# Two images, two stages at once: additive attention of one image beside the experts of the other

## The chip, the cores and the metric

The kernel runs on one core of one Trainium2 chip. The metric is the device time of one execution in microseconds (us). The core has five engines that take their instructions from queues of their own, in order: TensorE (PE in the profile; its weight loads are PEld), VectorE (DVE), ScalarE (ACT), GpSimd (POOL) and SyncE (SP), which here only starts transfers. POOL starts the indirect transfers (gathers and scatters by a list of rows).

## The reference, cut to what matters

The input is x with 2 images, 256 channels and 32 x 32 positions, in float32. Four layers follow each other. Layers 0 and 1 are attention over channels-first images and are not touched. Layers 2 and 3 work on tokens, 1024 an image, 256 values each:

```python
t = _to_tokens(x)
t = t + _L2_attn_ref(_ln_t(t), ...)      # attention in windows of 64 tokens
t = t + _L2_ffn_ref(_ln_t(t), ...)       # 8 experts, top 2, hidden width 1024
t = t + _L3_attn_ref(_ln_t(t), ...)      # additive attention, within one image
t = t + _L3_ffn_ref(_ln_t(t), ...)       # 8 experts, top 2, hidden width 512

# _L3_attn_ref, U = 32 units
q = inputs @ Wt;  k = inputs @ Wx
h = tanh(q[:, :, None, :] + k[:, None, :, :] + bh)   # 2 x 1024 x 1024 x 32 values
a = softmax(h @ Wa + ba);  v = a @ inputs

# an expert layer, for each token and its two experts
h = gelu(xf @ W1 + b1);  y = h @ W2 + b2;  out = sum of weight * y
```

Every step here works within one image, so the two images do not depend on each other from layer 2 on.

## The kernel before, in words

All matrix work is float32. A tile is 128 tokens; there are 16 (NT), eight an image. Each stage treats both images and ends before the next one begins, because the next norm needs its result. From layer 2 on the order is: norm, `window_attention`, norm, `route`, `experts` (layer 2), norm, `additive_attention`, norm, `route`, `experts` (layer 3) with `finish`, which writes the output.

*Experts.* `route` computes the gate, picks two experts a token and gives every token-expert pair a row ("slot") in a buffer in HBM, sorted by expert and padded so that a tile of TILE = 256 slots belongs to one expert: NTILES = 23 tiles. The tokens are scattered to `slots_in` by 32 indirect transfers (L934). For each tile, `fetch` gathers the whole weights of its expert with one indirect transfer (L952: 2.10 MB in layer 2, 1.05 MB in layer 3) and loads the tokens on SP (L964); `turn` transposes them (L973) and in layer 2 applies the expert's scale and shift on VectorE (L979); `up` does the first matrix product (L992) and `gelu` on ScalarE with the bias in the same instruction (L996); `down` does the second product (L1005), VectorE copies it (L1009) and SP stores it to `slots_out` (L1010). The weights have three buffers. The order of this loop is fixed by hand: within `tc.manual_schedule()` every engine's queue has the order in which the program emits. Elsewhere a scheduler orders the instructions by priority (the order of the program) and by its own estimate of when they are ready. At the end 32 gathers (L1031) bring the two results of each token back, and VectorE adds them with their shares (L1035).

*Additive attention.* Keys lie with 32 units x 4 copies on the partitions, so one ScalarE instruction computes tanh for 4 queries against 1024 keys (L1109). A step is four of these; after eight steps a tile of 128 queries is done. TensorE sums over the units with the matrix `pick` (L1115, four column groups of 32); VectorE takes the maximum (L1120), ScalarE the exponential (L1125), TensorE transposes (L1133), VectorE copies (L1135), TensorE multiplies with the tokens (L1138), VectorE adds to t (L1142). The norms take their root on ScalarE (L79).

Of the kernel before, what the change touches and what calls it, by code (L numbers as in the profile page):

```python
# [19 lines left out]
F32 = mybir.dt.float32  # L20
U32 = mybir.dt.uint32
# [15 lines left out]
TILE = 256  # L37

NTILES = 2 * T // TILE + E - 1
MASKED = -1.0e30  # L40

# [6 lines left out]
class Stack:  # L48
# [351 lines left out]
    def layer0(self, xT):  # L400
        tc, nc = self.tc, self.nc
        with ExitStack() as ctx:
# [106 lines left out]
            for m in range(NTILES * TILE // P):  # L509
                nc.gpsimd.dma_start(out=self.slots_in[m * P : (m + 1) * P, :], in_=zero)  # L510
# [165 lines left out]
    def window_attention(self, t, u, uT):  # L676
# [124 lines left out]

    def route(self, pool, psum, uT, wr, br, normalise):

        nc = self.nc  # L810
        shape = [P, NT, E]
        tl = lambda name, s=shape, dt=F32: pool.tile(s, dt, name=name)
        ps = psum.tile(shape, F32, name="ps_router", tag="tr")
        for i in range(NT):
            for c in range(CC):
                nc.tensor.matmul(
                    ps[:, i, :], lhsT=uT[:, c, i * P : (i + 1) * P], rhs=wr[:, c, :],
                    start=(c == 0), stop=(c == CC - 1),
                )
        iota = lambda t, pattern, base, step: nc.gpsimd.iota(  # L820
            t, pattern=pattern, base=base, channel_multiplier=step, allow_small_or_imprecise_dtypes=True
        )
        rank, limits, tiles, part = tl("rank", [P, E]), tl("rt_lim", [P, E]), tl("rt_til", [P, NTILES]), tl("rt_part", [P, 1])
        iota(rank, [[-1, E]], E, 0)
        iota(limits, [[TILE, E]], 0, 0)
        iota(tiles, [[1, NTILES]], 0, 0)
        iota(part, [[0, 1]], 0, 1)

        before, ones = tl("rt_before", [P, P]), tl("rt_ones", [P, P])
        nc.gpsimd.memset(ones, 1.0)  # L830
        nc.gpsimd.affine_select(
            before, ones, pattern=[[1, P]], compare_op=ALU.is_ge, fill=0.0, base=-1, channel_multiplier=-1
        )
        over_tokens = lambda a, s=shape: a.unsqueeze(1).to_broadcast(s)
        one = tl("rt_one", [P, NT])
        lg, p, eq, h0, h1 = (tl(f"rt_{n}") for n in ("lg", "p", "eq", "h0", "h1"))
        nc.vector.tensor_tensor(lg, ps, over_tokens(br), ALU.add)
        nc.vector.tensor_reduce(one, lg, AX.X, ALU.max)
        nc.vector.tensor_tensor(lg, lg, broadcast(one, shape), ALU.subtract)
        nc.scalar.activation(lg, lg, AF.Exp)  # L840
        nc.vector.tensor_reduce(one, lg, AX.X, ALU.add)
        nc.vector.reciprocal(one, one)
        nc.vector.tensor_tensor(p, lg, broadcast(one, shape), ALU.mult)
        left = p
        for hot in (h0, h1):
            nc.vector.tensor_reduce(one, left, AX.X, ALU.max)
            nc.vector.tensor_tensor(eq, left, broadcast(one, shape), ALU.is_equal)
            nc.vector.tensor_tensor(eq, eq, over_tokens(rank), ALU.mult)
            nc.vector.tensor_reduce(one, eq, AX.X, ALU.max)
            nc.vector.tensor_tensor(hot, over_tokens(rank), broadcast(one, shape), ALU.is_equal)  # L850
            if hot is h0:
                nc.vector.scalar_tensor_tensor(lg, hot, -2.0, p, ALU.mult, ALU.add)
                left = lg
        both = eq
        nc.vector.tensor_tensor(both, h0, h1, ALU.add)


        flat = lambda a: a.rearrange("p n e -> p (n e)")
        inside = psum.tile(shape, F32, name="ps_before", tag="before")
        nc.tensor.matmul(flat(inside), lhsT=before, rhs=flat(both), start=True, stop=True)  # L860
        counts = psum.tile(shape, F32, name="ps_counts", tag="counts")
        nc.tensor.matmul(flat(counts), lhsT=ones, rhs=flat(both), start=True, stop=True)
        a, b, n = tl("rt_a"), tl("rt_b"), 1
        nc.vector.tensor_copy(a, counts)
        while n < NT:
            nc.vector.tensor_copy(b[:, :n], a[:, :n])
            nc.vector.tensor_tensor(b[:, n:], a[:, n:], a[:, : NT - n], ALU.add)
            a, b, n = b, a, 2 * n
        total = a[:, NT - 1, :]
        over, need = tl("rt_over", [P, E, E]), tl("rt_need", [P, E])  # L870
        nc.vector.tensor_tensor(
            over, broadcast(total, [P, E, E]), over_tokens(limits, [P, E, E]), ALU.is_gt
        )
        nc.vector.tensor_reduce(need, over, AX.X, ALU.add)
        ends, spare, n = tl("rt_ends", [P, E]), tl("rt_spare", [P, E]), 1
        nc.vector.tensor_copy(ends, need)
        while n < E:
            nc.vector.tensor_copy(spare[:, :n], ends[:, :n])
            nc.vector.tensor_tensor(spare[:, n:], ends[:, n:], ends[:, : E - n], ALU.add)
            ends, spare, n = spare, ends, 2 * n  # L880
        nc.vector.tensor_tensor(spare, ends, need, ALU.subtract)
        nc.vector.tensor_scalar(spare, spare, float(TILE), None, ALU.mult)
        nc.vector.tensor_tensor(b, a, counts, ALU.subtract)
        nc.vector.tensor_tensor(b, b, inside, ALU.add)
        nc.vector.tensor_tensor(b, b, over_tokens(spare), ALU.add)
        slots, shares = [], []
        for n, hot in enumerate((h0, h1)):
            nc.vector.tensor_tensor(lg, hot, b, ALU.mult)
            nc.vector.tensor_reduce(one, lg, AX.X, ALU.add)
            slots.append(tl(f"rt_slot{n}", [P, NT], U32))  # L890
            nc.vector.tensor_copy(slots[n], one)
        whose, index = tl("rt_whose", [P, NTILES, E]), tl("rt_index", [P, NTILES])
        shape_t = [P, NTILES, E]
        nc.vector.tensor_tensor(whose, over_tokens(ends, shape_t), broadcast(tiles, shape_t), ALU.is_le)
        nc.vector.tensor_reduce(index, whose, AX.X, ALU.add)
        nc.vector.tensor_scalar(index, index, float(E - 1), float(P), ALU.min, ALU.mult)
        nc.vector.tensor_scalar(index, index, part, None, ALU.add)
        rows = tl("rt_rows", [P, NTILES], U32)
        nc.vector.tensor_copy(rows, index)

        nc.vector.tensor_tensor(p, p, both, ALU.mult)
        if normalise:
            nc.vector.tensor_reduce(one, p, AX.X, ALU.add)
            nc.vector.reciprocal(one, one)
            nc.vector.tensor_tensor(p, p, broadcast(one, shape), ALU.mult)
        for n, hot in enumerate((h0, h1)):
            nc.vector.tensor_tensor(hot, hot, p, ALU.mult)
            shares.append(tl(f"rt_share{n}", [P, NT]))
            nc.vector.tensor_reduce(shares[n], hot, AX.X, ALU.add)
        return p, shares, slots, rows  # L910

    def experts(self, t, u, routes, packed, b2, hid, affine, finish=lambda g: None):

        tc, nc = self.tc, self.nc  # L920
        HB, TB = hid // P, TILE // P
        weights, shares, slots, rows = routes
        width = packed.shape[1]
        with ExitStack() as ctx:
            sb = ctx.enter_context(tc.tile_pool(name="ex_sb", bufs=2))
            wp = ctx.enter_context(tc.tile_pool(name="ex_w", bufs=3))
            p_x = ctx.enter_context(tc.tile_pool(name="ex_x", bufs=2, space=PSUM))
            p_h = ctx.enter_context(tc.tile_pool(name="ex_h", bufs=2, space=PSUM))
            p_y = ctx.enter_context(tc.tile_pool(name="ex_y", bufs=2, space=PSUM))
            xs, ys = self.slots_in, self.slots_out  # L930

            for i in range(NT):
                for slot in slots:
                    nc.gpsimd.indirect_dma_start(  # L934
                        out=xs, out_offset=bass.IndirectOffsetOnAxis(ap=slot[:, i : i + 1], axis=0),
                        in_=u[:, i, :], in_offset=None,
                    )

            for i in range(NT):
                ps = p_y.tile([E, P], F32, name="ps_wT", tag="ps_y")  # L940
                nc.tensor.transpose(ps, weights[:, i, :], self.ident)
# [72 lines left out]
            with tc.manual_schedule():  # L1014
# [4 lines left out]
                for m in range(NTILES):  # L1019
                    if m + 2 < NTILES:  # L1020
                        fetch(m + 2)
# [130 lines left out]
    def run(self):  # L1152
        tc, nc, ins = self.tc, self.nc, self.ins
        with ExitStack() as ctx:
# [29 lines left out]
            def norm(src=t, dst=u, dstT=uT):  # L1184
                self.layer_norm(dst, src, 1e-5)
                if dstT is None:
                    return
# [121 lines left out]
```

## Time and profile before

| | us |
|---|---|
| median of 3 runs | 3524.49 (3524.22 to 3526.67) |
| the profiled execution, own time | 3520.51 |
| its span, first to last instruction | 3518.8 |
| layers 0 and 1, with the turn to tokens | to about 1809 |
| window attention | 1809 to 2003 |
| norm, route, scatters | 2003 to 2142 |
| experts of layer 2 | 2142 to 2497 |
| gathers, norm, projections | 2497 to 2562 |
| additive attention | 2562 to 3138 |
| norm, route, scatters | 3138 to 3268 |
| experts of layer 3 | 3268 to 3468 |
| gathers and output | 3468 to 3519 |

The stages are read from the chain of work that ended last. Over the whole span TensorE is busy 88%, ScalarE 58%, VectorE 49%, POOL 7%. A busy share counts the time in which an instruction of the engine is under way; a matmul counts from its start to its modelled end, so matmuls with waits between them can look like a busy engine. The granted clock of TensorE is given as a share of full speed (mean 0.927 here).

### The profile page before, as it was taken

To read this page: it belongs to the slowest core of one execution; us is meant where nothing else is said; L and a number is where in the kernel's file an instruction comes from. 1 tells how busy PE (TensorE), PEld (TensorE's weight loads), DVE (VectorE), ACT (ScalarE), POOL (GpSimd) and SP (SyncE) were. 2 spreads that over 40 slices of the span, in tenths; PEclk is the share of its full clock that TensorE was granted. 3 is DMA by queue.
4 is the path that set the end of the run, shared out by engine and by line. 5 is a ranking of instruction groups with operands and counts; after the bars stand their busy time and mean duration, and the time that the engine had idled before them with its cause. 6 is when DMAs were issued, how large, how long until landed. Compare 5 with 4: busy or idle time off the path is not lost.

```text
span 3518.8 us, 67832 instructions
## 1 busy us (share of the span) xinstructions
PE 3106.9 (88%) x28148; PEld 1875.6 (53%) x28148; DVE 1725.4 (49%) x3134; ACT 2056.3 (58%) x3148; POOL 259.1 (7%) x411
## 2 busy tenths in 40 slices
PE   7999999999999989999979835999499999982795
PEld 4566665666656656656757714788322222231673
DVE  5989898898988945434545430111321111121112
ACT  2888888787888846646633201222189999950121
POOL 3000000000000000000000021000300000003113
PEclk9999999999999999999987657999799999985897
DMA  3000000000000000000000022444200000002454
GB/s 110 3 3 3 3 3 3 3 3 3 3 3 3 3 25 1 1 1 1 1 19 1 1 102 87 180 173 166 82 1 1 1 1 0 1 1 76 139 183 135
DMA packets 154356, 134.18 MB, mean 38 GB/s; under 512 B 114544, under 2 KB 141056, under 8 KB 148160
## 3 DMA queue, kind: packets, MB, share of 16 engines
q0 software_dynamic: 14976, 95.36, 7.2%
q1 hardware_dynamic: 137632, 34.02, 4.5%
q8 instruction: 221, 3.62, 0.4%
q14 instruction: 87, 0.71, 0.1%
q10 hardware_dynamic: 1440, 0.47, 0.1%
HBM read 100.51 MB, written 28.57 MB: 37 GB/s over the span
## 4 chain that ended last, share of the span: by engine, by line
PE 83%; DMA 6%; DVE 5%; issue 3%; ACT 2%; POOL 1%; SPq 0%; POOLq 0%; ACTq 0%; DVEq 0%
PE ps_s L272 13%; PE ps_o L348 13%; PE ps_e L1115 12%; PE ps_h L992 7%; PE ps_y L1005 7%; DMA slots_in<-u,rt_slot 4%; PE ps_t L330 4%; PE ps_s L143 4%; PE ps_o L210 3%; PE ps_t L173 3%; PE ps_v L1138 2%; PE ps_t L631 2%; PE ps_av L776 1%; DMA got<-slots_out,rt_slot 1%; PE ps_out L526 1%
## 5 line engine op out<-in xcount | busy, mean ns | idle before, releaser
L309 ACT ACTIVATE sc<-sc,sa_shift 128x1024 f32<-128x1024 f32 x512 | 585.2, 1148 | 53.1 <-DMA sa_shift<-sa_min 52.9
L1109 ACT ACTIVATE th<-kT,qb 128x1024 f32<-128x1024 f32 x512 | 535.2, 1134 | 8.5 <-DVE kT L1088 6.9
L272 PE MATMUL ps_s<-kT,qT 64*32 64x512 f32 x8192 | 503.9, 595 | 9.2 <-ACT sc L282 8.5
L348 PE MATMUL ps_o<-wt,v 128*64 128x128 f32 x6144 | 502.2, 276 | 0.0
L1115 PE MATMUL ps_e<-th,pick 128*32 128x512 f32 x2048 | 470.7, 602 | 0.9 <-DVE kT L1088 0.9
L322 DVE STREAM_TRANSPOSE wt<-sc 128x768 f32<-128x768 f32 x512 | 465.7, 943 | 1.0 <-ACT sc L309 1.0
L348 PEld LDWEIGHTS ps_o<-wt,v 128*64 128x64 f32 x6144 | 441.2, 137 | 42.5 <-issue 42.5
L996 ACT ACTIVATE h<-ps_h,w 128x256 f32<-128x256 f32 x276 | 130.6, 473 | 477.2 <-PE ps_h L992 477.2
L282 ACT COPY sc<-ps_s 128x1024 f32<-128x1024 f32 x256 | 257.4, 1005 | 116.1 <-PE ps_s L272 42.4
L293 DVE TENSOR_REDUCE sa_least<-sc 128x1 f32<-128x1024 f32 x256 | 306.1, 1196 | 1.4 <-ACT sc L282 1.3
L279 DVE TENSOR_SCALAR_CACHE_REDUCE sc<-ps_s 128x1024 f32<-128x1024 f32 x256 | 301.3, 1177 | 5.9 <-PE ps_s L272 5.9
L992 PE MATMUL ps_h<-xe,w 128*128 128x256 f32 x1104 | 253.4, 387 | 35.0 <-issue 31.0
L1115 PEld LDWEIGHTS ps_e<-th,pick 128*32 128x32 f32 x2048 | 93.0, 108 | 333.0 <-ACT th L1109 227.1
L1009 DVE COPY y<-ps_y 128x256 f32<-128x256 f32 x92 | 39.0, 424 | 453.3 <-PE ps_y L1005 453.3
L348 PE MATMUL ps_o<-wl,v_odd 128*64 128x128 f32 x2048 | 250.9, 276 | 0.0
L1005 PE MATMUL ps_y<-w,h 128*128 128x256 f32 x1104 | 245.5, 379 | 0.0
L992 PEld LDWEIGHTS ps_h<-xe,w 128*128 128x128 f32 x1104 | 196.5, 191 | 84.8 <-issue 40.6
L149 DVE TENSOR_SCALAR_CACHE_REDUCE sc<-ps_s 128x1024 f32<-128x1024 f32 x128 | 151.6, 1222 | 178.5 <-PE ps_s L143 178.5
L272 PEld LDWEIGHTS ps_s<-kT,qT 64*32 64x32 f32 x8192 | 126.9, 106 | 200.6 <-issue 169.5
L1005 PEld LDWEIGHTS ps_y<-w,h 128*128 128x128 f32 x1104 | 210.2, 190 | 28.1
L330 PEld LDWEIGHTS ps_t<-ident,sc 128*128 128x128 f32 x1024 | 107.3, 140 | 215.7 <-issue 168.5
L348 PEld LDWEIGHTS ps_o<-wl,v_odd 128*64 128x64 f32 x2048 | 220.3, 137 | 0.0
(248 smaller groups left out, 3525.3 us busy)
## 6 DMA issues: line engine op xcount, KB each, us to landing
xr<-slots_in SPq DMA_DIRECT2D x46, 256.0 KB, 2.8
slots_out<-y SPq DMA_DIRECT2D x46, 256.0 KB, 2.2
sa_got<-sa_least SPq DMA_DIRECT2D x512, 0.5 KB, 1.8
sa_shift<-sa_min SPq DMA_DIRECT2D x512, 0.2 KB, 1.7
slots_in<-zero POOLq DMA_DIRECT2D x46, 128.0 KB, 2.2
sa_sums<-sa_total SPq DMA_DIRECT2D x256, 1.0 KB, 1.8
xT<-in_x SPq DMA_DIRECT2D x4, 496.0 KB, 4.2
sb_l_w_in<-in_l_w_in SPq DMA_DIRECT2D x1, 1536.0 KB, 6.3
```

The source lines that it names most:

```text
L272: nc.tensor.matmul(ps[r][S * c : S * (c + 1), a, :].rearrange("p (b i) -> p b i", i=S), lhsT=qT[half, p, S * i : S * (i + 1)], rhs=keys[ha ...
L279: nc.vector.tensor_scalar(scores[m][0], flat[0], 1.0, None, ALU.mult, ALU.min, accum_out=least[m // 2][:, 0, h : h + 1])
L282: nc.scalar.copy(scores[m][1], flat[1])
L293: nc.vector.tensor_reduce(least[m // 2][:, 1, h : h + 1], scores[m][1], AX.X, ALU.min)
L309: nc.scalar.activation(scores[m][r], scores[m][r], AF.Exp, bias=shift[m // 2][:, r : r + 1], scale=-1.0, accum_out=total[i][:, 2 * p + r, ...
L322: nc.vector.transpose(weights[i, h][:, 2 * p + r, :], scores[m][r][:, :DIRECT])
L330: nc.tensor.transpose(ps[:, g, r, :], s[:, at : at + P], self.ident)
L348: nc.tensor.matmul(sums[i][64 * k : 64 * (k + 1)], lhsT=values, rhs=w, start=(h == 0 and j == 0 and t == 0), stop=(h == 1 and j == 1 and t ...
L992: nc.tensor.matmul(ps, lhsT=a[:, c, j * P : (j + 1) * P], rhs=x[:, c, :], start=(c == 0), stop=(c == CC - 1),)
L1005: nc.tensor.matmul(ps, lhsT=h[:, j, k * P : (k + 1) * P], rhs=b[:, j, :], start=(j == 0), stop=(j == HB - 1),)
L1109: nc.scalar.activation(h, keys.rearrange("p (a b) -> p a b", a=2), AF.Tanh, bias=qb[:, i, g : g + 1])
L1115: nc.tensor.matmul(pe[c * U : (c + 1) * U, a, :], lhsT=pick[:, k, :], rhs=h[:, a, :], start=(k == 0), stop=(k == G - 1),)
```

## The change

From layer 2's experts on, each stage is cut by image. A new class `Late` holds the stages as generators that emit a piece of work and yield. `run` gives each one a start, an end and a number of pieces, and emits the pieces of all in the order of these places, all inside one `manual_schedule`. So the experts of image 0 run beside the dispatch (norm, route, scatter) of image 1; the attention of image 0 beside the experts of image 1; the attention of image 1 beside the layer-3 dispatch, experts and collect of image 0; the same for image 1 comes last. The dispatch of image 0 in layer 2 is emitted inside `window_attention`, after the last tile of image 0.

With it come these edits. The expert tile is 128 slots (TILE = 128), with 23 tiles an image. A gelu takes its bias from a VectorE add before it, covers 512 values, and is emitted one `up` later. `fetch`, `turn` and `up` have a new order. Slots have a buffer for each image. The root in the norms is computed on VectorE (`inverse_root`, three Newton steps on the bits), not on ScalarE. The exponentials of attention come in batches of 4, 3 and 1 tiles. The buffer of sums `ps_e` is single, tanh tiles have eight buffers as before. Constants are loaded when layer 2 begins.

```diff
-TILE = 256
-NTILES = 2 * T // TILE + E - 1
+IT = N // P
+TILE = 128
+NTILES = 2 * N // TILE + E - 1
...
+                after(i, lambda shape, name: p_mm.tile(shape, F32, name=name, tag="ps_mm"))
...
+            late = Late(ctx, self, t)
...
+                def after(i, psum):
+                    if i == IT - 1:
+                        late.misc = psum
+                        for _ in late.dispatch(2, 0):
+                            pass
+                self.window_attention(t, u, uT, after)
+            late.run()
...
+    def inverse_root(self, var, eps):
...
+        for step in range(3):
+            nc.vector.scalar_tensor_tensor(a, y, -0.5, y, ALU.mult, ALU.mult)
+            nc.vector.tensor_tensor(a, a, x, ALU.mult)
+            nc.vector.scalar_tensor_tensor(y, a, 1.5, y, ALU.add, ALU.mult)
...
+    def dispatch(self, l, b):
+        for half in range(2):
+            yield from self.normed(b, half)
+        yield from self.route(l, b)
+        u = self.u[b]
+        if l == 2:
+            yield from self.norm(lambda i: u[:, i, :], lambda i: u[:, i, :], range(IT))
+        p, shares, slots, rows = self.routes[l, b]
+        nc, t = self.nc, self.t
+        for i in range(IT):
+            for slot in slots:
+                nc.gpsimd.indirect_dma_start(
+                    out=self.stack.slots_in[b],
...
+        yield
+        for i in range(IT):
...
+            nc.tensor.matmul(ps, lhsT=wT, rhs=self.b2[l], start=True, stop=True)
...
+    def experts(self, l, b):
...
+        def fetch(m):
+            w = sb.tile([P, WIDEST], F32, name="ew", bufs=3)
+            nc.gpsimd.indirect_dma_start(
...
+            raw[m] = sb.tile([P, C], F32, name="xr", bufs=3)
+            nc.sync.dma_start(out=raw[m], in_=xs[m * TILE : (m + 1) * TILE, :])
...
+        def activate():
+            while waiting:
+                to, x = waiting.pop()
+                nc.scalar.activation(to, x, AF.Gelu)
+        def up(m, k):
...
+            h = sb.tile([P, 4, TILE], F32, name="hb")
+            nc.vector.tensor_tensor(h, ps, broadcast(b1[:, 4 * k : 4 * k + 4], [P, 4, TILE]), ALU.add)
+            activate()
+            waiting.append((hidden[m][:, 4 * k : 4 * k + 4, :], h))
...
+        fetch(0)
+        fetch(1)
+        yield
+        turn(0)
+        turn(1)
+        yield
+        for k in range(HB // 4):
+            up(0, k)
+            yield
+        for m in range(NTILES):
+            if m + 2 < NTILES:
+                fetch(m + 2)
+            if m + 1 < NTILES:
+                for k in range(HB // 4):
+                    up(m + 1, k)
+                    if k == 0 and m + 2 < NTILES:
+                        turn(m + 2)
+                    yield
...
+            down(m)
+            yield
...
+    def additive(self, b):
...
+        batches = {3: range(4), 6: range(4, 7), 7: range(7, 8)}
+        for s in range(IT * G + 1):
+            if s < IT * G:
+                tanh(s)
+            if s > 0:
+                products(s - 1)
+                if s % G == 0 and s // G - 1 in batches:
+                    softmax(batches[s // G - 1])
+            yield
+            if jobs:
+                jobs.pop(0)()
...
+        self.p_x, self.p_h, self.p_y, self.p_e = psum("lt_x", 1), psum("lt_h", 2), psum("lt_y", 1), psum("lt_e", 1)
+        plan = [
+            (self.experts(2, 0), 0, 185, 72),
+            (self.dispatch(2, 1), 5, 110, 28),
+            (self.collect(2, 0), 186, 225, 18),
+            (self.experts(2, 1), 186, 480, 72),
+            (self.additive(0), 226, 535, 65),
+            (self.collect(2, 1), 482, 525, 18),
+            (self.additive(1), 536, 850, 65),
+            (self.dispatch(3, 0), 552, 620, 24),
+            (self.experts(3, 0), 625, 790, 50),
+            (self.collect(3, 0), 795, 840, 11),
+            (self.dispatch(3, 1), 880, 900, 24),
+            (self.experts(3, 1), 905, 1000, 50),
+            (self.collect(3, 1), 1001, 1040, 11),
+        ]
+        heap = [(start, k) for k, (_, start, _, _) in enumerate(plan)]
+        with self.tc.manual_schedule():
+            while heap:
+                heap.sort()
+                at, k = heap.pop(0)
+                step, start, end, pieces = plan[k]
+                if next(step, False) is None:
+                    heap.append((at + (end - start) / pieces, k))
```

The jobs of `additive` are the transposes and the product with the tokens of one tile, one job after each step. `collect` gathers an image's results eight rows of transfers ahead, adds them, and then in layer 2 norms and projects half an image at a time for the attention, in layer 3 writes the output. `b` is the image, `l` the layer, `m` the expert tile, a block of 128 slots. The numbers in `plan` only fix the order.

## The prediction

> **What bounds the kernel now.** I read the windows view by stage first, then the groups, then the chain, then single stretches of the timeline. The windows view (the reader is to see which engine fills each stage):
>
> ```profile
> core 0: us, PE busy (x) PEld busy (x) DVE busy (x) ACT busy (x) POOL busy (x), PEclk, DMA share, GB/s
> 2160.00:2497.00 337.00, 322.54 (x1511) 271.22 (x1509) 40.03 (x88) 82.13 (x174) 18.93 (x20) 1.00 0.42 158
> 2497.00:2552.00 55.00, 5.29 (x27) 4.18 (x28) 29.88 (x86) 2.90 (x5) 30.82 (x33) 0.57 0.31 86
> 2552.00:3130.00 578.00, 562.19 (x2454) 153.81 (x2452) 71.89 (x150) 556.25 (x548) 0.88 (x6) 1.00 0.00 1
> 3182.00:3268.00 86.00, 17.15 (x34) 6.38 (x33) 7.13 (x23) 1.28 (x1) 31.86 (x33) 0.50 0.21 82
> 3268.00:3468.00 200.00, 176.82 (x828) 148.27 (x828) 35.41 (x69) 43.56 (x92) 18.94 (x20) 0.98 0.48 165
> 3468.00:3518.80 50.80, 10.95 (x32) 4.62 (x32) 15.47 (x32) 4.29 (x8) 30.49 (x32) 0.53 0.43 129
> ```
>
> The expert stages (337, 200) are TensorE's with ScalarE a quarter busy; the attention (578) is ScalarE's. Its PE "busy" of 562 is matmuls spread out by waiting: the group lines and two runs show the real rates.
>
> ```profile
> L1109 ACT ACTIVATE th<-kT,qb 128x1024 f32<-128x1024 f32 x512 | 535.2, 1134 | 8.5 <-DVE kT L1088 6.9
> L996 ACT ACTIVATE h<-ps_h,w 128x256 f32<-128x256 f32 x276 | 130.6, 473 | 477.2 <-PE ps_h L992 477.2
> ```
>
> The next are a timeline line, then four of the chain (start, us, what):
>
> ```profile
> 2614.65 10.48 ACT L1109 ACTIVATE th<-kT,qb 128x1024 f32<-128x1024 f32 x10
> ...
> 1701.88 1.77 PE ps_t L173 x16
> ...
> 2202.45 7.17 PE ps_h L992 x32
> 2209.62 6.91 PE ps_y L1005 x32
> ...
> 2609.38 1.85 PE ps_e L1115 x14
> ```
>
> Ten tanh in 10.48 us is 1.04 each back to back, so a step (four) holds ScalarE 4.16. The same step's 16 matmul records, once its inputs are there, run in about 1.85 (14 of them recorded): TensorE is needed 44% of that stage. 32 records of 256 columns take 6.9 to 7.2 (216 ns each); 16 of 128 columns with 128-column weights take 1.77 (110 ns each).
>
> The gaps between stages are the third part: 32 scatters, each waiting on POOL for the one before, then the gathers.
>
> ```profile
> 2099.70 0.97 POOL L934 DMA_INDIRECT slots_in<-u,rt_slot  x1 [1.68 <-DMA slots_in<-u,rt_slot]
> 2102.34 0.97 POOL L934 DMA_INDIRECT slots_in<-u,rt_slot  x1 [1.68 <-DMA slots_in<-u,rt_slot]
> ...
> w<-in_l_packed,rt_rows POOLq DMA_INDIRECT x20, 8.6
> w<-in_l_packed,rt_rows POOLq DMA_INDIRECT x20, 5.9
> ```
>
> A scatter costs 2.64. The last two lines are weight fetches, issue to landing: 8.6 in layer 2 (2.10 MB), 5.9 in layer 3 (1.05 MB), so 388 GB/s behind a fixed 3.2. From the end of window attention (2003) to the end is 1516 us.
>
> **What the Trainium skill says.** "DMA: Bandwidth & Descriptors", Specifications, puts HBM at about 358 GB/s for a core; the slope above (388) is near. "ScalarE: Activation LUTs", Table sets, puts Tanh in Exp's set and in Sigmoid's; the trace agrees on the first (Exp follows Tanh at L1125 with no load). Its section on table loads gives 1283 ns and a drain of 1380; the trace has 1283 and no gap behind it. "TensorE: Matmul & The Clock Gate", Back-to-back issue gap, says weight loads can set the spacing at 128 columns, 81 ns where columns alone give 56 (1.45 times); the 110 above already has such loads in it.
>
> **The change, part by part.** New stages in order, from the rows above.
>
> 1. *Image 0's dispatch inside window attention.* The second half of that stage lasts 104; DVE is busy 94 of 194, leaving some 54. The dispatch adds about 45 on DVE: three norms of eight tiles at 0.5 + 0.33 each, 36 small Newton operations at 0.17, some 45 route operations at 0.25, copies and the b2 adds (8 x 0.7). It fits, but in a DVE-ACT-PE chain: I take **+25** (0 if all falls in gaps, 50 if none does and POOL's t adds queue behind scatters). Its 16 scatters (42) end about with the stage. End 2028.
>
> 2. *Experts 2 of image 0, beside the dispatch of image 1.* Tokens do not grow: 46 blocks of 128 for 23 tiles of 256. Up is 32 records of 128 columns, 3.5 (at 1.45 times 5.1); down 3.46; turn 0.25: 7.25 a block against 7.6 for half an old tile. But each block fetches all 2.10 MB: **weight traffic doubles**. fetch(m+2) needs the buffer that down(m-1) frees and is needed right after down(m): two blocks take a landing plus a block's work, 8.6 + 0.9 (POOL, two landings overlapping) + 0.8 (turn) + 7.25, so 8.8 a block (floor by bytes, rows and results with it, 6.1; PE 7.25). First block 17, then 22 x 8.8: 210. VectorE's new bias add (0.69, as the 128x512 copy at L983) twice a block is covered: DVE's own work is 2.6 a block. SP's load (2.8) and store (2.2) per block are short of 8.8 too. The dispatch puts 16 scatters into POOL in one piece, with the fetches behind: 42 less the 7 that POOL would wait anyway: +35. **245** (205 with scatters hidden, 280 at landings of 12).
>
> 3. *Collect image 0, start experts of image 1.* Store 2.7, eight gathers at 1.26 ahead of the fetches on POOL, then 8.6: w is there after 23, the second after 27. DVE waits for both in the early turns, with the gathered adds queued behind; then adds, two half norms, transposes, projections, some 33: **60** (40 to 70).
>
> 4. *Attention of image 0 beside the rest of those experts.* Up to the last expert piece: 53 attention pieces, 20.3 blocks. ScalarE: 53 x 4.16 + 41 gelus x 0.55 + 4 exps and loads (8) = 251. TensorE: 53 x 1.85 + 20.3 x 7.25 + 4 x 4.4 (turn and values) = 263. Two queues in fixed order with tanh buffers two steps deep cannot both be full: a gelu now stands behind four tanh, and a down behind the gelu; ps_e has one buffer, so each eighth step waits for its evacuation (1.2, L1120); DVE, waiting in turn for the landing, holds up ps_e and ptT. I take +10%, 290 (nothing to +30%). The last 12 steps with the collect beside: 65. **355** (320 to 410).
>
> 5. *Attention of image 1 beside layer 3 of image 0.* ScalarE: 64 x 4.16 + 23 gelus x 0.55 + exps and loads 19 = 298. TensorE: 64 x 1.85 + 8 x 4.4 + 23 x 3.75 + 25 = 265. ScalarE bounds; +5% and 11 where PE stands at the first turn behind 16 scatters: **325** (300 to 380).
>
> 6. *The tail, nothing beside it.* Dispatch 36 (43 before, half the tiles but the same number of operations); scatters 42, fetches now behind all of them; first block 9. Then a block is (5.9 + 0.5 + 3.75)/2 = 5.1, not PE's 3.75: 22.5 x 5.1 = 115. Collect 16 gathers, 20, with 11 for store and output. **233** (205 to 265).
>
> Sum 2028 + 245 + 60 + 355 + 325 + 233 = 3246 (+5 for the change of pools: 3251). Against the same execution's 3518.8 that is 268 less; its own time was 3520.5 (1.7 more), the median 3524.5 (4.0 above that). So **3257**. Table loads: each of six exp batches and two router exps amid gelus costs two, 2.6, counted. Tanh beside gelu without a load is not in the trace: between nothing and 1.28 a switch; I take nothing, since the page finds Tanh packed in two sets.
>
> **The rivals.**
> *Overlap half lost.* Each queue stands behind the other's late producer: stages 4 and 5 go half-way to the sum of both engines' work (stage 4: 263 and 251 to 388, +100; stage 5: +40). For it: one DVE queue serves both and waits for landings. Against: the waits are shorter than the 12 us of a merged block. 3397.
> *Fetches and scatters hide.* If the landing overlaps better and POOL's scatters cost little, stage 2 is 185, 3 is 40, 4 is 320, 6 is 205: 3257 - 143 = 3114. For it: 388 GB/s would carry a block in 6.1. Against: POOL stood for every scatter in the trace.
> *A table load at every turn from tanh to gelu and back.* 64 gelus x 2 x 1.28 = 164, all on ScalarE where it bounds: 3417.
> *Slower: the granted clock.* If TensorE, busy in bits between waits, gets less clock in stages 2, 4 and 5, its 165 + 263 + 265 grow. At 0.65 stage 4's first part is 263/0.65 x 1.1 = 445 (+155), 5 is 428 (+103), 2 some +40: 298, past the 268 saved, so **3555**; at 0.7 it would still win. For it: window attention has 0.73 with PE "busy" 90%, and Part 1 of that TensorE page halves the clock after some 3.4 us of idling. Against: the attention stage has 1.00 with PE waiting half the time.
> That the merged order is not what is executed is hardly possible: both engines take it from one fixed list.
>
> **How the numbers follow.** Forecast 0.60, half lost 0.20, hidden 0.11, loads 0.04, clock 0.05. Range 3100 to 3420: it takes in the hidden case, half-lost and loads; the clock and the sum of all worst bounds (some 3480) are outside. Faster by over 0.2% (about 7 us, what a measurement of this kernel can tell) 0.94, within it 0.01, slower 0.05: every case but the low clock is faster by over 100.
>
> **What would show it.** Right: layer 2's experts alone at 8.5 to 9 us a block with PE waiting for w or xe; a hole of some 35 in them while POOL scatters; tanh and matmul both over 80% busy at clock 1.00 in stages 4 and 5; some 72 MB more read (46 fetches more, 23 of 2.10 and 23 of 1.05); a tail of about 230 with PE half idle. Wrong: table loads by the dozen, merged stages over 400, a clock under 0.8, or no hole at the scatters.

## The result, and the profile after

The kernel after takes 3834.64 us (median of 4 runs, 3830.10 to 3845.10) against 3524.35 (4 runs, 3516.09 to 3526.67): ratio 1.0889, 95% interval 1.0860 to 1.0918. It is **slower by about 310 us**, where 267 less was forecast. The profiled execution has a span of 3834.9, mean granted clock 0.889.

The page of the kernel after, first the activity in 40 slices of 96 us (the experts and attention start in slice 22), then the groups and transfers around the experts:

```profile
PE   7999999999999899998885446566777876876454
ACT  2888888888888465564311000025566785562000
PEclk9999999999999899999867767778898888887777
...
L1299 ACT ACTIVATE th<-kT,qb 128x1024 f32<-128x1024 f32 x512 | 541.8, 1135 | 302.2 <-PE ps_e L1308 282.6
L1140 PE MATMUL ps_x<-ident,xr 128*128 128x128 f32 x184 | 55.6, 400 | 501.6 <-DMA xr<-slots_in 474.8
...
xr<-slots_in SPq DMA_DIRECT2D x92, 128.0 KB, 6.9
HBM read 173.05 MB, written 28.57 MB: 53 GB/s over the span
```

Neither engine is full in any of the last 19 slices. In the groups the number ahead of the last arrow is idle time ahead of such instructions, the one behind it what was waited for most. TensorE stands 474.8 us for the token load `xr` at the small transposes of `turn` (L1140); ScalarE's tanh stands 282.6 for TensorE's sums. The load, half as large as before, lands 6.9 us after its issue (a median over the 24 of the 92 whose landing the profile gives). In the kernel before it took 2.8:

```profile
xr<-slots_in SPq DMA_DIRECT2D x46, 256.0 KB, 2.8
```

The read volume shows that the change is what the diff says: 173.05 MB against 100.51 before, 72.5 more.

The windows of the new stages, with the columns of the prediction's windows view (stretch and its length; busy us of PE, PEld, DVE, ACT and POOL with their instructions; granted clock, DMA share, GB/s):

```profile
2027.00:2475.00 448.00, 239.94 (x1225) 214.48 (x1226) 94.60 (x278) 32.95 (x50) 37.66 (x40) 0.74 0.34 126
2547.00:2940.00 393.00, 283.95 (x1780) 174.62 (x1782) 62.62 (x126) 230.42 (x240) 17.86 (x19) 0.88 0.32 115
3030.00:3490.00 460.00, 357.58 (x1995) 180.26 (x1994) 106.02 (x281) 301.75 (x306) 52.81 (x55) 0.87 0.23 78
3570.00:3803.00 233.00, 130.70 (x598) 112.49 (x598) 35.36 (x69) 14.47 (x23) 20.51 (x22) 0.78 0.39 129
```

In the first stage TensorE is busy about half the time and DMA a third. So the weights' bandwidth is not the limit: the same column reached 0.42 and 158 GB/s before.

One block of image 0's layer-2 experts in the timeline of the kernel after (start, duration, what; in brackets the idle time ahead of it and its releaser):

```profile
2288.97 0.42 DVE L1181 COPY y<-ps_y 128x256 f32<-128x256 f32 x1 [4.83 <-PE ps_y L1177]
2289.21 0.94 POOL L1123 DMA_INDIRECT ew<-in_l_packed,rt_rows  x1 [22.47 <-PE ps_wT L996]
2289.43 0.32 SPq L1182 DMA_DIRECT2D slots_out<-y  x1
2289.84 0.38 SPq L1135 DMA_DIRECT2D xr<-slots_in  x1
2290.26 2.05 PE L1164 MATMUL ps_h<-xe,ew 128*128 128x128 f32 x16
2298.15 0.69 PE L1140 MATMUL ps_x<-ident,xr 128*128 128x128 f32 x2 [5.84 <-DMA xr<-slots_in]
2298.63 3.62 PE L1164 MATMUL ps_h<-xe,ew 128*128 128x128 f32 x16
2304.44 5.15 PE L1177 MATMUL ps_y<-ew,h 128*128 128x256 f32 x16
```

These eight lines show how a block loses its time. The load of block m+2 is emitted behind the store of y(m-1). So SP starts it 0.63 us after the fetch of m+2 (2.10 MB), and it lands 8.3 us later, with the fetch (the trace has the last mark of the fetch's landing at 2297.92 and the load's at 2298.11). Its transposes stand on TensorE right behind the first half of up(m+1). The second half and down(m), which need nothing of those tokens, stand behind them and start when the load lands. The next fetch waits for the end of that down. **One** block takes a whole landing and its work: without the dispatch beside it fetches follow each other by 17.1 us (2396.11, 2413.15, 2430.34, 2447.38), where 8.8 was forecast. Coming out of such a pause the second half of up takes 3.62 and down 5.15, where the same 16 records take 2.05 and 3.62 elsewhere.

The same in the merged stage, on both engines:

```profile
2712.72 1.92 PE L1308 MATMUL ps_e<-th,pick 128*32 128x512 f32 x16
2714.72 4.26 ACT L1299 ACTIVATE th<-kT,qb 128x1024 f32<-128x1024 f32 x4 [2.49 <-PE ps_e L1308]
2724.16 0.69 PE L1140 MATMUL ps_x<-ident,xr 128*128 128x128 f32 x2 [7.54 <-DMA xr<-slots_in]
2727.97 7.38 ACT L1299 ACTIVATE th<-kT,qb 128x1024 f32<-128x1024 f32 x7 [8.47 <-PE ps_e L1308]
```

The attention's own matmuls stand behind the same transposes. ScalarE runs out of free tanh tiles and stands 8.47 us for products whose inputs were there: the four tanh end at 2718.98, and the products over them start only at 2724.78, behind the transposes.

### The profile page after: what moved, and what is told of

The parts are those of the page before. It is cut to its first block, busy times and chain, and to the rows that moved or that the text cites. A ratio compares the mean times of both kernels' runs of the same rounds, so it can differ in the third digit from the quotient of the medians.

```text
span 3834.9 us, 70941 instructions
## 1 busy us (share of the span) xinstructions
PE 3074.1 (80%) x29260; PEld 1981.9 (52%) x29260; DVE 1888.6 (49%) x3650; ACT 2002.7 (52%) x2990; POOL 302.2 (8%) x451
## 3 DMA queue, kind: packets, MB, share of 16 engines
HBM read 173.05 MB, written 28.57 MB: 53 GB/s over the span
## 5 line engine op out<-in xcount | busy, mean ns | idle before, releaser
L1299 ACT ACTIVATE th<-kT,qb 128x1024 f32<-128x1024 f32 x512 | 541.8, 1135 | 302.2 <-PE ps_e L1308 282.6
L314 ACT ACTIVATE sc<-sc,sa_shift 128x1024 f32<-128x1024 f32 x512 | 585.1, 1148 | 51.5 <-DMA sa_shift<-sa_min 51.3
L1154 ACT ACTIVATE h<-hb 128x512 f32<-128x512 f32 x138 | 85.9, 623 | 733.8 <-DVE hb L1169 730.7
L1140 PE MATMUL ps_x<-ident,xr 128*128 128x128 f32 x184 | 55.6, 400 | 501.6 <-DMA xr<-slots_in 474.8
L1164 PEld LDWEIGHTS ps_h<-xe,ew 128*128 128x128 f32 x2208 | 314.1, 224 | 55.9 <-issue 47.2
L1308 PE MATMUL ps_e<-th,pick 128*32 128x512 f32 x2048 | 330.7, 694 | 3.3 <-ACT th L1299 2.3
L1164 PE MATMUL ps_h<-xe,ew 128*128 128x128 f32 x2208 | 324.2, 309 | 2.1 <-DVE hb L1169 2.1
L1177 PE MATMUL ps_y<-ew,h 128*128 128x256 f32 x1104 | 305.6, 434 | 1.2 <-DVE y L1181 1.2
L1140 PEld LDWEIGHTS ps_x<-ident,xr 128*128 128x128 f32 x184 | 24.7, 187 | 519.2 <-DMA xr<-slots_in 316.3
L1177 PEld LDWEIGHTS ps_y<-ew,h 128*128 128x128 f32 x1104 | 236.2, 222 | 75.2 <-issue 36.4
L1169 DVE TENSOR_TENSOR hb<-ps_h,ew 128x512 f32<-128x512 f32 x138 | 95.2, 691 | 305.5 <-PE ps_h L1164 286.9
```

The costliest lines, as they stand in the source:

```text
L314: nc.scalar.activation(scores[m][r], scores[m][r], AF.Exp, bias=shift[m // 2][:, r : r + 1], scale=-1.0, accum_out=total[i][:, 2 * p + r, ...
L1164: nc.tensor.matmul(ps[:, j, :], lhsT=a[:, c, at : at + P], rhs=x[:, c, :], start=(c == 0), stop=(c == CC - 1),)
L1177: nc.tensor.matmul(ps, lhsT=h[:, j, :], rhs=w2[:, j, :], start=(j == 0), stop=(j == HB - 1))
L1299: nc.scalar.activation(h, keys, AF.Tanh, bias=self.qb[b][:, s // G, g : g + 1])
L1308: nc.tensor.matmul(pe[i][c * U : (c + 1) * U, a, :], lhsT=self.pick[:, k, :], rhs=h[:, a, :], start=(k == 0), stop=(k == G - 1),)
```

## The experiments

The main theory: token loads that land late, on TensorE's queue. The rivals: the doubled weight fetches themselves, the smaller tile, or the merging. All kernels are the kernel after with the edit shown, except the last of this section. A time without a range is one run, except for e10 (two).

**e1, the load earlier.** It is started two blocks ahead, in five buffers.

```diff
-            raw[m] = sb.tile([P, C], F32, name="xr", bufs=3)
+        def load(m):
+            raw[m] = sb.tile([P, C], F32, name="xr", bufs=5)
             nc.sync.dma_start(out=raw[m], in_=xs[m * TILE : (m + 1) * TILE, :])
...
         fetch(0)
         fetch(1)
+        for m in range(4):
+            load(m)
...
             if m + 2 < NTILES:
                 fetch(m + 2)
+            if m + 4 < NTILES:
+                load(m + 4)
```

> The change with one thing moved: the token load of block m+4 (five buffers, not three) is started where that of block m+2 was, so it is two blocks early. Theory A (each block's tokens are loaded behind the store of the block before and beside 2.1 MB of weights, land about 8.4 us later, and TensorE stands in its queue at the transpose until then; in the merged stages ScalarE stands with it): TensorE's 475 us of waiting for xr goes, TensorE's clock comes back, and the stages fall to what the prediction had: 3250 to 3350. Rival B (two engines in one fixed order hold each other up, tokens or not): only the unmerged stages (experts of image 0 in layer 2, the tail) gain, some 300: 3530. Rival C (twice the weights are too many bytes): the wait moves from xr to ew, gain under 150: above 3690.

3400.85 (3390.93 to 3404.74, 4 runs), ratio to before 0.9678 (0.9648 to 0.9708): 434 less than the kernel after, by the load's start alone. It still lands in 6.8 us, but TensorE's wait for it falls from 474.8 to 57.5. The time lies 51 above the range of theory A, and below those of both rivals. The waits of e1 (engine, line, what is waited for: us in all, times, longest):

```profile
DVE xe L1146 <- DMA ew<-in_l_packed,rt_rows: 268.2, 41, 50.0
PEld ps_b L1000 <- DVE wT L998: 98.6, 32, 54.5
ACT th L1305 <- PE ps_e L1314: 69.3, 34, 9.0
PE ps_x L1142 <- DMA xr<-slots_in: 57.5, 6, 33.3
```

Now `turn` itself waits, on VectorE, for the scale and shift, which come with the weights. Beside the dispatch this holds up that stage's b2 pieces (L998, L1000). Away from it, two lines of e1's timeline show the block that was forecast:

```profile
2271.47 0.95 POOL L1123 DMA_INDIRECT ew<-in_l_packed,rt_rows  x1 [16.13 <-PE ps_y L1179]
...
2288.78 0.94 POOL L1123 DMA_INDIRECT ew<-in_l_packed,rt_rows  x1 [9.12 <-DVE xe L1146]
```

One fetch lies between (2278.72): two blocks in 17.3, 8.7 each.

**e2, the store out of the load's way.** One word: POOL starts the store.

```diff
-            nc.sync.dma_start(out=ys[m * TILE : (m + 1) * TILE, :], in_=y)
+            nc.gpsimd.dma_start(out=ys[m * TILE : (m + 1) * TILE, :], in_=y)
```

> The change with one word edited: the store of y is started by POOL, not by SP, so that SP's queue holds only token loads and runs ahead as far as three buffers let it. Theory A with the order on SP as its reason (the load stands behind the store of the block before): nearly the gain of e1, less what POOL's store delays the next fetch (about 0.5 us a block): 3280 to 3420. If instead the landing is slow whenever weights are under way, wherever the load stands in its queue, little changes: above 3700.

3482.43, above the range. The load lands in a median 2.2, and TensorE's wait for it falls to 51.5. But the fetch now stands on POOL behind a store that waits for VectorE's copy (POOL stands 733.1 us at these stores), and VectorE waits 336.7 us for weights: the wait moved to the other queue.

**e3, without the weights' traffic.** Only the first three fetches of each image and layer are made.

```diff
-            w = sb.tile([P, WIDEST], F32, name="ew", bufs=3)
+            if m < 3:
+                kept.append(sb.tile([P, WIDEST], F32, name="ew", bufs=3))
...
+            w = kept[m % 3]
```

> Leaves out the weight fetches but the first three of each experts call; later blocks use those buffers again. Token loads stay as late as in the change. Theory A (the landing of 8.4 us is mostly the queue of weight bytes in the same DMA engines): xr lands in about 2.8 as before the change, TensorE's wait for it falls from 475 to under 120 us, and with no fetch to wait for the time is 3250 to 3350. If the late start alone makes the wait and the bytes do not matter, landing stays near 7 and the time above 3650.

3298.99, in the range. The load lands in 2.1. TensorE's wait for it falls to 124.4, just above the 120 expected. So it is the large transfers beside it that make 6.9 of it. Leaving these fetches out is worth 536, the waits for the weights included; e1 got 434 with all of them in place.

**e4, the turn later.** The load starts and lands as late as ever (6.1), but its transposes stand behind down(m).

```diff
-                    if k == 0 and m + 2 < NTILES:
-                        turn(m + 2)
...
             down(m)
+            if m + 2 < NTILES:
+                turn(m + 2)
```

> The change with turn(m+2) emitted after down(m), not after the first up of block m+1; loads stay where they are. Theory A (the place of the transpose on TensorE's queue, ahead of an up and a down that do not need it, is what makes the landing cost): the landing now runs beside up and down; a block alone takes (9.3 + 1.3 + 7)/2, some 8.8 us, so 3280 to 3420, though TensorE still waits for xr in the unmerged stages. If the order does not matter (B or C), within 60 of 3835.

3363.36, in the range: 471 less with the same transfers in the same order. TensorE's wait for tokens is 98.8, tanh's for TensorE 73.7. So most of what the late load costs comes through what stands behind it on TensorE.

**e5, both.** The edits of e1 and e4.

> The early token load of e1 and the late turn of e4 together. Theory A, as e1 and e4 left it: with tokens there in time, the next thing that a queue stands for is VectorE's scale and shift of turn(m+2), which waits for the weights that were started one block before, with the dispatch's small VectorE pieces (and TensorE's b2 products) behind it; the late turn puts that wait behind the block's own work. The parts add for the most part: experts of image 0 from 331 in e1 to about 275, attention of image 0 as in e4 (335), tail as in e1 (258): 3290 to 3340. If both edits cured only the same wait, it stays at e4's level: 3355 or more.

3338.02 (3334.43 to 3349.44, 4 runs), ratio 0.9503 (0.9471 to 0.9535), at the upper edge of the range; clock 0.936. Its windows, stage by stage as above:

```profile
2027.00:2312.00 285.00, 200.72 (x1224) 178.09 (x1224) 93.77 (x279) 32.97 (x50) 35.29 (x37) 0.88 0.53 197
2375.00:2720.00 345.00, 325.86 (x2196) 202.14 (x2195) 96.97 (x225) 298.15 (x310) 33.18 (x35) 0.98 0.39 138
2720.00:3073.00 353.00, 315.44 (x1960) 165.92 (x1958) 100.07 (x273) 298.79 (x304) 52.80 (x55) 0.94 0.31 101
```

The clock is back with the waits gone (0.74 to 0.88, 0.88 to 0.98). In the merged stages ScalarE is now busy 85 to 86% of the time (298.15 of 345, 298.79 of 353).

**e6 and e9, the scatters spread.** e5 with the dispatch's scatters two at a time between its b2 pieces (a `yield` and a second loop head fewer), so that fetches come between them. e9 is the same kernel with four runs.

> e5 with the 16 scatters of a dispatch issued two at a time with the eight b2 pieces, not all in one piece. Theory A with the prediction's hole (fetches stand behind 16 scatters on POOL, about 41 us in the change): the hole spreads over four blocks, but POOL's time (2.6 a scatter) stays and fetches are what bounds there, so 10 to 30 less than e5. If the hole was not POOL's, no change; over 20 more than e5 if POOL waits of two scatters hit each fetch in the merged stages.

> The kernel of e6 again, now beside the kernel before in three rounds: from that one look (3324.5), 3318 to 3335, ratio 0.944 to 0.949. If e6's gain of 13.5 us on the version with both repairs was only scatter between executions, 3334 to 3349.

e6 took 3324.48, 13.5 under e5 and in its range. e9 took 3315.90 (3306.47 to 3331.99, 4 runs), ratio 0.9413 (0.9389 to 0.9437), just under its range and below e5's interval. It is the **fastest version here**, 5.9% under the kernel before. From e9's first fetch (2039.24) to the first gather is 269.7, where e5 has 288.4; but the same edit delays image 0's own dispatch, and that fetch comes 15 later, so little of this remains by the gathers. The traced execution of e9 is the slowest of its four (3331.99), 2.4 us under that of e5 (3334.43), so the trace can't show where most of the gain came in.

**e10, the dispatch first.** In e5's plan image 1's dispatch goes ahead of image 0's experts.

> The version with both repairs (e5), with image 1's layer-2 dispatch put ahead of image 0's experts, not beside them. Its first expert stage (first fetch to first gather) took 288 us, where the prediction's sum was 245 with 35 for the scatter hole. Theory that blocks cost 8.8 us when their tokens are there and what is left over comes from work of the dispatch in the same queues: the stage, now alone, takes 200 to 220. Rival that the blocks themselves are slower than summed (weight landings of 10 us and more): 245 or more. Either way the dispatch, no longer covered (some 80 to 95 us), costs more than is won: 3345 to 3390 in all.

3354.94 (3352.16 and 3357.72), in the range. The dispatch takes 88 uncovered (first fetch at 2112.68, in e5 at 2024.35). The experts' stage takes 219.7, from 2112.68 to 2332.41, and its fetches follow by 9.1. So blocks are near the forecast when alone. Of e5's 288.4, 69 come with the dispatch's instructions in the same queues. 46 of these are the hole in which POOL scatters: e5's fetches at 2115.34 and 2170.40 lie 55 apart, less a block's 9.

**e7, the merging taken out.** e1 with a plan in which no attention lies beside experts. Layer 3 comes behind both attentions, with the dispatch of image 1 beside the experts of image 0.

> e1 with another plan and nothing else: the two attentions come one after the other behind both layer-2 experts, with no experts beside them, and layer 3 follows. What it tells: what the merging of attention and experts is worth once tokens come in time. Theory A (merging works, the cost was the token wait): slower than e1 by the experts' time that is hidden there, 200 to 300: 3600 to 3700. Rival B (merged queues hold each other up so that little is hidden): within 80 of e1's 3401.

3685.09, in the range of theory A: the merging is worth 284 us once the tokens are there, net of the new order in layer 3. It is not what made the change slow.

**e8, the tile alone.** The kernel *before* with `TILE = 128` and nothing else (39 tiles).

> The kernel before with TILE = 128 and nothing else: 39 tiles of 128 for 23 of 256, so 39 weight fetches a layer for 23, in the old order (turn(m+1) a block after its loads). Theory A: bytes alone cost little: two blocks take a landing and a block's work, 8.8 and 5.1 a block, 39 x 8.8 = 343 for layer 2 (355 now with its start) and 199 for layer 3 (200): 3500 to 3560. Rival C (twice the weight traffic is what makes the change slow): 3700 or more.

3560.10, some 43 above before on the same chip (3517.05), at the edge of the lower range. So the smaller tile, with 16 more fetches a layer (the change has 23 more), is a small part of the loss.

**e11 and e12, the order of two lines.** In both POOL starts the token load, in e11 ahead of the block's fetch, in e12 right behind it. No store stands on that queue.

e11:

```diff
+            nc.gpsimd.dma_start(out=raw[m], in_=xs[m * TILE : (m + 1) * TILE, :])
...
             nc.gpsimd.indirect_dma_start(
...
-            nc.sync.dma_start(out=raw[m], in_=xs[m * TILE : (m + 1) * TILE, :])
```

e12:

```diff
-            nc.sync.dma_start(out=raw[m], in_=xs[m * TILE : (m + 1) * TILE, :])
+            nc.gpsimd.dma_start(out=raw[m], in_=xs[m * TILE : (m + 1) * TILE, :])
```

> The changed kernel with one thing moved: POOL, not SP, starts the token load, immediately ahead of the block's weight fetch; the turn stays where it is. Its counterpart e12 has the same two transfers on POOL in the other order. Theory that a load lands late because it comes behind the fetch: here it lands in 2 to 3 us, TensorE waits about 1 us a block for it, the fetch starts 0.9 us later: 3360 to 3450. Rival that the place on SP behind the store, or the turn's place on TensorE alone, is enough for the loss: above 3700 in both.

> As e11, but POOL starts the token load right behind the fetch (some 1.2 us after the fetch's start), with no store ahead of it on its queue. Theory that coming behind the fetch makes it late: landing of 6 us or more, TensorE's wait for tokens near the 475 us of the changed kernel, 3800 to 3900. Rival that the place on SP behind the store, or the slot in SP's ring, made it late: landing of 2 to 3 and 3360 to 3450, as in e11.

3415.86 and 3843.41, both in the range of the main theory: 428 us by two lines changing places. The first line is from e11's waits, the second from e12's:

```profile
PE ps_x L1140 <- DMA xr<-slots_in: 111.4, 6, 48.2
```

```profile
PE ps_x L1140 <- DMA xr<-slots_in: 542.3, 87, 48.6
```

In e12 a load issued at 2281.95, 0.96 after its fetch, lands at 2289.67, 7.7 later: neither SP nor the store ahead of it is needed to make it late (on POOL it waits in the fetch's own queue, as the last section shows; e2 has late loads on SP with no store there). In two points my expectation for e11 was wrong. The load doesn't wait for the weight buffer: POOL starts it right behind the *previous* block's fetch (2289.07, then 2290.05), and its own fetch follows 7.7 later (2297.78). And it doesn't land in 2 to 3 us: the last mark of its landing in the trace is at 2297.98, 7.9 after its start. It lands late too, but a block early, as e1's is two blocks early, and TensorE waits for it only 6 times. The pair therefore shows what an early start is worth, not that a load ahead of a fetch lands fast.

## Why the prediction was wrong

The stages in the prediction's cuts, from the timelines (first fetch, first gather, first tanh, last projection of the second attention, which lies 14.5 ahead of its first tanh, last tanh, end):

| step | predicted | after | e5 |
|---|---|---|---|
| 1 dispatch inside window attention, end at | 2028 | 2028 | 2024 |
| 2 experts of image 0 beside dispatch | 245 | 451 | 288 |
| 3 collect and start | 60 | 68 | 63 |
| 4 attention of image 0 beside experts | 355 | 484 | 345 |
| 5 attention of image 1 beside layer 3 | 325 | 448 | 353 |
| 6 tail | 233 | 356 | 259 |

The column after sums to 3835, 589 above the forecast's 3246; 581 of them lie in the four steps that have expert blocks in them.

*The step that failed* is the sentence in step 2 that "SP's load (2.8) and store (2.2) per block are short of 8.8 too". It took the load's 2.8 from the kernel before, where the load starts 0.17 after the fetch (median); in the kernel after the load takes 6.9 (the last section shows why). The step left out two things that the diff shows: that the load now starts behind the store of y(m-1), which puts it 0.63 after the fetch; and that the turn stands ahead of half an up and of a down on TensorE. With a landing of 6.9 to 8.3 the "two blocks take a landing plus a block's work" becomes one block: 17.1 alone, where 8.8 was forecast, and 92 blocks are built this way. e1 and e11 (the load early) and e4 (the turn late) each remove one of these two faults and win 419 to 471; with both removed (e5) the same steps hold within 43 us each. None of the three rivals of the forecast nor the slow one was this. "Overlap half lost" comes nearest, since in it too a queue stands behind a late producer, but it was priced in the merged stages alone, and one of its terms was wrong: half-way from 298 to the sum of 298 and 265 is 430, which adds 105 to stage 5, not 40, so by its own rule it stood at 3462, not 3397. The range missed because every case shared the term. Of the forecast's own signs of being wrong, merged stages over 400 (484 and 448) and a clock under 0.8 (0.74) came.

*Step 1* was right: 2027.7. *Step 3* was right within 8.

*The scatter hole of step 2* was right. The POOL timeline of the kernel after:

```profile
2167.52 0.94 POOL L1123 DMA_INDIRECT ew<-in_l_packed,rt_rows  x1 [16.11 <-PE ps_y L1177]
2180.79 1.00 POOL L987 DMA_INDIRECT slots_in<-u,rt_slot  x1 [12.32 <-DVE u L946]
...
2225.72 0.99 POOL L1123 DMA_INDIRECT ew<-in_l_packed,rt_rows  x1 [0.30 <-issue]
```

58.2 between two fetches, where the blocks around it take 17: 41, predicted 35.

*The weight traffic* was right in volume (72.5 MB, predicted 72), and so was its price: 8.7 and 9.1 a block in e1 and e10, predicted 8.8. What was missing beside it, some 23 us (69 less the hole of 46 in e5), came with the dispatch too; the wait of the b2 pieces in e1 points to its other work in the same queues, but no run isolates it.

*Steps 4 and 5* were right as soon as tokens came in time (e5: 10 under and 28 over, or 4 and 14 over when the cut is at the second attention's first tanh). The 10% taken for two full queues was about enough.

*The tail* was sized at 5.1 a block. The kernel after has 10.6 (fetches at 3690.45 and 3700.94, 19 intervals in 200.95), e5 5.6 (19 in 106.30): 10 of e5's 26 over. The rest was not isolated.

*The table loads* of that rival did not come (its time was 4 short: 3257 and 164 make 3421). "ScalarE: Activation LUTs", Table sets, packs Tanh with Exp and with Sigmoid and says nothing of Tanh beside Gelu. Here 138 gelus lie among 512 tanh; the gelus need 6 loads, the exps 4, the tanh none. So taking nothing was right, but by luck: neither of the two sets that the forecast gave as its reason is Gelu's.

```profile
L1154 ACT ACT_TABLE_LOAD x6 | 7.7, 1283 | 21.2 <-DVE hb L1169 21.1
L1326 ACT ACT_TABLE_LOAD x4 | 5.1, 1283 | 0.1
```

*The clock.* It fell, to 0.74 in step 2 and to 0.88 and 0.87 in steps 4 and 5, but not to the 0.65 of that rival, and behind the waits rather than as their cause: every repair raised it. "TensorE: Matmul & The Clock Gate", Part 1, has idle windows of about 3.4 us take the clock away. The trace agrees: the pauses shown here last 5.8 to 7.5, and down takes 5.15 soon after one and 3.62 elsewhere.

## What to carry to other kernels

Price a transfer by what starts beside it, not by its size alone: the landing of a small load in one kernel holds in the next only while it keeps its place against the large one. Then ask what stands behind the first instruction that needs it, on an engine that works in order, and put there only what needs it too. Start small loads a block early where buffers allow (e1, e11), or put their consumer behind the independent work (e4); either alone gave back over 70% of the loss against the forecast (434 by e1, 471 by e4, 497 by both in e5), since neither fault costs much without the other.

## What the runs showed of the hardware that was not expected

How late a 128 KB load lands turns on tenths of a microsecond. Started a median 0.17 us after the start of a large fetch (256 KB, before) it lands in 2.8, and 0.63 after (in the kernel after) in 6.9; without fetches it takes 2.1. e2, where SP starts no stores of y, has loads of both kinds. Its 19 loads that start 0.36 to 0.39 after a fetch land in a median 2.0, 2.5 to 6.3 ahead of that fetch. Of its 31 that start 0.8 to 8.3 after a fetch still under way, 27 land within 0.6 behind it. In e1, 58 loads start 0.63 to 7.65 after such a fetch, and land a median 0.2 (at most 1.5) behind that fetch, whenever they started. Where between 0.39 and 0.63 the change lies was not tried.

The packets of the block shown above (2289.21) tell what goes on. From 2293 to 2297 us its two queues moved (packets, MB, share of the 16 DMA engines' time):

```profile
q0 software_dynamic: 96, 1.53, 89.4%
q1 hardware_dynamic: 99, 0.10, 6.9%
```

q0 has the fetch, in packets of 16 KB, and q1 the load, in packets of 1 KB. Almost as many packets of one move as of the other: the two take turns packet by packet, not byte by byte. Each has 128 packets of data, so they end together, although the load has a sixteenth of the bytes. A load can also be ahead of all this: in e2 one starts at 2301.38, 0.39 behind its fetch, and its packets move from 2302.33 to 2302.91, while the fetch's begin at 2302.82. On POOL the load goes into the fetch's own queue: in e12 its packets start at 2288.33, when the fetch's last start at 2288.37.

"Trainium Kernel Development and Optimization", Key Constraints, says that the transfers of SP, ACT and POOL run on the same 16 DMA engines and interleave. The trace agrees (96 packets beside 99), and shows what this means for a small load beside a large one: with as many packets, it ends as late.
